# Moving one feed-forward layer of a four-chunk transformer and state-space kernel from beside an attention stage to the kernel's tail

## The chip, the core and the metric

The kernel runs on one core of a Trainium2 chip. The core has five engines, each with its own instruction queue that is worked off in order: TensorE (PE, matmuls; PEld is its loading of weights), VectorE (DVE), ScalarE (ACT), GpSimd (POOL) and SyncE (SP, which issues most of the DMAs here). Data for the engines is in SBUF, and matmul results land in the eight banks of PSUM. The metric is the device time of one execution, in microseconds; lower is better.

## The reference

The input x is float32 of shape (2, 1024, 256): two sequences of 1024 tokens with 256 features. Four layers follow one another, each with a residual:

```python
x = x + attention(layernorm(x))        # 16 heads of 128, causal mask and a linear position bias
x = x + ternary_ffn(layernorm(x))      # silu(gate) * up, 1024 wide, weights at three levels, RMS norm
x = x + mamba(layernorm(x))            # state space: 512 channels, 16 states, recurrence over the tokens
x = x + kept_two_ffn(layernorm(x))     # silu(gate) * up, 1024 wide; of each 4 values the 2 largest stay
```

In the last layer the choice is made by the absolute values of four neighbouring features:

```python
h = silu(x @ w_gate) * (x @ w_up)
h_sparse = sparsify_2to4(h)            # keeps the two of each four with the largest |h|
out = h_sparse @ w_down
```

The recurrence of the third layer is `h = dA * h + dbu`, `y = sum over the states of h * c`, token by token; attention is causal. So the first half of a sequence doesn't depend on the second half, in any layer.

## The kernel before

The tokens are cut into four chunks of 512 (`CH`: two sequences, two halves each; `U` = 512). The residual of a chunk stays in SBUF as `x[k]`. Everything is written in plain Python loops, so the program is one long list of instructions. A scheduler fixes each engine's order before the run: the order in the source is its priority, and it may pull ready work of a later place ahead. It also adds the waits, and hands out buffers: a tile with the tag of an earlier one takes its buffer when the last reader is done.

**Stages.** `attention()` is a generator that yields after each block of 128 queries of a head, 64 times a chunk (16 heads, 4 blocks). `rest(k)` is a second generator with the other three layers of chunk k: `ternary_ffn`, `state_space`, `kept_two_ffn`. The main part at the end of the function interleaves the two: stage 0 is the attention of the first chunk, beside the quantization of weights; in stage k (1 to 3) the attention of chunk k (counted from 0) runs beside `rest(k - 1)`. After stage 3 the attention's pools are closed (`actx.close()`), and `rest(3)` runs alone: the tail.

**Pace.** Each `yield` of `rest` names a cost in planned units. `REST` is their sum, 296.4: 227.6 for the ternary layer and the state space, and 68.8 for the last layer. After block i of 64, `rest` is advanced until it has spent REST * (i + 1) / 64.

**The layer that is moved, `kept_two_ffn` (L671).** It loads three weights of 1 MB each on SP (L679, L681, L683), normalizes and transposes `x[k]` (`layernorm_T`, tile `xT_g`), then for each of 8 pieces calls `glu`: four matmuls for the gate and four for the up half as the profile counts them (L398, tiles `g_g` and `u_g`), a silu on ACT (L403, `sg_g`), and a product on DVE (L404, into `gh`). For every second piece ACT takes absolute values (L700, `ab`). DVE compares these (six comparisons, L706, `cm`), applies four rules (L718, L719, L720: `wins`, `gh`), and the output matmuls (L727, `go`) are added to the residual on DVE (L732, `o`) and stored. All its tiles lie in pools on the right side of SBUF; its PSUM banks come from `ps_r`.

**PSUM.** Two banks with tag s (`ps_s`, attention's scores, and the decay factors of the last chunk's scan), three with tag mm (`ps_mm` and `ps_z`, attention), one y, two r (`ps_r`, shared by all layers of `rest`).

**The state space's scan loop (from L569).** 4 channel groups times 16 states give 64 products. For each one `spread` loads two broadcast rows into `bcs` (512 KB, L576, on SP), `factors` makes the decay `da` on ACT (L593) and the drive `db` (L596: on POOL; in the last chunk two of three on DVE), `scan` runs the recurrence on DVE (L603, `hs`), `weigh` multiplies by the second row on POOL (L614, `hc`), and `total` adds the result into the bank `y` by four PE transposes (L583). `gate` closes a group of 16; at the end `mo` (L663) projects back. `tail_end` is true for the last chunk alone; it selects deeper buffers (`bcs` 8 rather than 5).

Of the kernel before, what the change touches and what calls it, by code (L numbers as in the profile page):

```python
# [9 lines left out]
F32 = mybir.dt.float32  # L10
# [7 lines left out]
P = 128  # L18
B, S, D = 2, 1024, 256
H, DH = 16, 128  # L20
# [5 lines left out]
NFC = FF // P  # L26
GRP = 64
DI, DN, DR, DC = 512, 16, 128, 4
NDC = DI // P
NX = DR + 2 * DN  # L30
U = 512
UT = U // P
# [10 lines left out]
def kernel(  # L43
# [28 lines left out]
    def bank(tag, bufs):  # L72
        return lambda name, dt=F32: ps.tile([P, 512], dt, tag=tag, name=name, bufs=bufs)


    ps_s, ps_mm, ps_z = bank("s", 2), bank("mm", 3), bank("mm", 3)
    ps_y, ps_r = bank("y", 1), bank("r", 2)


    CH = [(b, u) for b in range(B) for u in range(NU)]  # L80
# [18 lines left out]
    def layernorm_T(k, key, put, bank):  # L99

        mv = ln.tile([P, UT, 2], F32, tag="mv", name=f"mv_{key}")
        for i in range(UT):
            st = ln.tile([P, 6], F32, tag="st", name=f"st_{key}_{i}", bufs=3)
            nc.vector.bn_stats(st, x[k][:, i, :])
            nc.vector.bn_aggr(mv[:, i, :], st)
        rstd = ln.tile([P, UT], F32, tag="rstd", name=f"rstd_{key}")
        nc.scalar.activation(rstd, mv[:, :, 1], AF.Sqrt, bias=ln_eps)
        nc.vector.reciprocal(rstd, rstd)
        for i in range(0, UT, 2):
            tp = bank(f"lnp_{key}_{i}").rearrange("p (c t) -> p c t", c=KC)  # L110
            for j in range(2):
                xn = ln.tile([P, D], F32, tag="xn", name=f"xn_{key}_{i}_{j}", bufs=2)
                nc.vector.tensor_scalar(
                    xn, x[k][:, i + j, :], mv[:, i + j, 0:1], rstd[:, i + j : i + j + 1],
                    ALU.subtract, ALU.mult,
                )
                for c in range(KC):
                    nc.tensor.transpose(
                        tp[:, c, j * P : (j + 1) * P], xn[:, c * P : (c + 1) * P], ident
                    )  # L120
            put(slice(i * P, (i + 2) * P), tp)

    def plain(pool, key):
        xT = pool.tile([P, KC, U], F32, tag="xT", name=f"xT_{key}")
        return xT, lambda t, p: nc.any.tensor_copy(xT[:, :, t], p)
# [72 lines left out]
    for h in range(H):  # L198
# [18 lines left out]
        fill=-MASKED, base=0, pattern=[[-1, P]], channel_multiplier=1,  # L217
# [171 lines left out]
    nc.scalar.activation(a_neg, cols_sb[:, :, DC : DC + DN], AF.Exp)  # L389
    nc.vector.tensor_scalar(a_neg, a_neg, -1.0, None, ALU.mult)  # L390

    def glu(pool, key, xTs, g_of, u_of, ic, h):

        g_ps, u_ps = ps_r(f"g_{key}_{ic}"), ps_r(f"u_{key}_{ic}")
        for p, w_of in ((g_ps, g_of), (u_ps, u_of)):
            for c in range(KC):
                for i, xT in enumerate(xTs):
                    nc.tensor.matmul(  # L398
                        p, lhsT=w_of(c, ic), rhs=xT[:, c, :],
                        start=(c == 0 and i == 0), stop=(c == KC - 1 and i == len(xTs) - 1),  # L400
                    )
        sg = pool.tile([P, U], F32, tag="sg", name=f"sg_{key}_{ic}", bufs=2)
        nc.scalar.activation(sg, g_ps, AF.Silu)  # L403
        nc.vector.tensor_tensor(h, sg, u_ps, ALU.mult)  # L404
# [63 lines left out]
    def state_space(k):  # L468
        b, u = CH[k]
        first, last, tail_end = u == 0, u == NU - 1, k == len(CH) - 1  # L470
        ps_da = ps_s if tail_end else ps_r
        with ExitStack() as mctx:
            mc = mctx.enter_context(tc.tile_pool(name="mc", bufs=1, side="right"))
            m2 = mctx.enter_context(tc.tile_pool(name="m2", bufs=2, side="right"))
# [15 lines left out]
            xT, put = plain(mc, f"m{k}")  # L490
# [79 lines left out]
            live, parts, yTs = {}, {0: steps(0)}, {}  # L570
            yield 3

            def spread(i):
                c, n = prods[i]
                live[i] = m2.tile([P, 2, U], F32, tag="bcs", name=f"bcs_{k}_{c}_{n}", bufs=8 if tail_end else 5)
                nc.sync.dma_start(  # L576
                    out=live[i], in_=bcd[:, n, :].unsqueeze(0).to_broadcast([P, 2, U])
                )
# [62 lines left out]
            for i in range(AHEAD):  # L641
                spread(i)
# [17 lines left out]
            for t in range(UT):  # L660
                op = ps_r(f"mo_{k}_{t}")
# [6 lines left out]
                nc.vector.tensor_tensor(xt, xt, op[:, :D], ALU.add)  # L668
                yield 2

    def kept_two_ffn(k):  # L671

        b, u = CH[k]
        W = 2 * U
        with ExitStack() as gctx:
            gc = gctx.enter_context(tc.tile_pool(name="gc", bufs=1, side="right"))
            g2 = gctx.enter_context(tc.tile_pool(name="g2", bufs=2, side="right"))
            wg_sb = gc.tile([P, KC, FF], F32, name=f"wg_sb_{k}")
            nc.sync.dma_start(out=wg_sb, in_=wg.rearrange("(c p) m -> p c m", p=P))  # L679
            wu_sb = gc.tile([P, KC, FF], F32, name=f"wu_sb_{k}")  # L680
            nc.sync.dma_start(out=wu_sb, in_=wu.rearrange("(c p) m -> p c m", p=P))  # L681
            wd_sb = gc.tile([P, NFC, D], F32, name=f"wd_sb_{k}")
            nc.sync.dma_start(out=wd_sb, in_=wd.rearrange("(c p) m -> p c m", p=P))  # L683
            out_dst = out[b, u * U : (u + 1) * U, :].rearrange("(t p) d -> p t d", p=P)
            xT, put = plain(gc, f"g{k}")
            layernorm_T(k, f"g{k}", put, ps_r)
            yield 3
            hT = gc.tile([P, NFC, U], F32, name=f"gh_{k}")
            ab = gc.tile([P, 4, W], F32, name=f"ab_{k}")

            h4 = hT.rearrange("p (j a) t -> p j (a t)", j=4)
            for ic in range(NFC):
                glu(
                    g2, f"g{k}", [xT],
                    lambda c, ic: wg_sb[:, c, ic * P : (ic + 1) * P],
                    lambda c, ic: wu_sb[:, c, ic * P : (ic + 1) * P],
                    ic, hT[:, ic, :],
                )
                if ic % 2:
                    nc.scalar.activation(ab[:, ic // 2, :], h4[:, ic // 2, :], AF.Abs)  # L700
                yield 4

            cm = gc.tile([P, 6, W], BF16, name=f"cm_{k}")
            pairs = [(0, 1), (0, 2), (0, 3), (1, 2), (1, 3), (2, 3)]
            for n, (i, j) in enumerate(pairs):
                nc.vector.tensor_tensor(cm[:, n, :], ab[:, i, :], ab[:, j, :], ALU.is_ge)  # L706
                yield 1.3
            beats = lambda i, j: cm[:, pairs.index((i, j)), :]

            rules = (  # L710
                (beats(0, 1), beats(0, 2), ALU.add, beats(0, 3), ALU.add, ALU.is_ge, 2.0),
                (beats(1, 2), beats(0, 1), ALU.subtract, beats(1, 3), ALU.add, ALU.is_ge, 1.0),
                (beats(2, 3), beats(0, 2), ALU.subtract, beats(1, 2), ALU.subtract, ALU.is_ge, 0.0),
                (beats(0, 3), beats(1, 3), ALU.add, beats(2, 3), ALU.add, ALU.is_le, 1.0),
            )
            for j, (a, c, op_a, d, op_b, cmp, least) in enumerate(rules):
                wins = g2.tile([P, W], BF16, tag="wins", name=f"wins_{k}_{j}")
                nc.vector.tensor_tensor(wins, a, c, op_a)  # L718
                nc.vector.tensor_tensor(wins, wins, d, op_b)  # L719
                nc.vector.scalar_tensor_tensor(  # L720
                    h4[:, j, :], wins, least, h4[:, j, :], op0=cmp, op1=ALU.mult
                )
                yield 2.5
            for t in range(UT):
                op = ps_r(f"go_{k}_{t}")
                for ic in range(NFC):
                    nc.tensor.matmul(  # L727
                        op[:, :D], lhsT=hT[:, ic, t * P : (t + 1) * P], rhs=wd_sb[:, ic, :],
                        start=(ic == 0), stop=(ic == NFC - 1),
                    )  # L730
                o = g2.tile([P, D], F32, tag="o", name=f"o_{k}_{t}", bufs=2)
                nc.vector.tensor_tensor(o, x[k][:, t, :], op[:, :D], ALU.add)  # L732
                nc.sync.dma_start(out=out_dst[:, t, :], in_=o)
                yield 4

    def rest(k):
        yield from ternary_ffn(k)
        yield from state_space(k)
        yield from kept_two_ffn(k)

    REST = 3 + 3 * NFC + 2 * UT + 3 + 4 * NDC + 4 + 3 * NDC + 2.2 * (DN * NDC + 4) + 2 * UT
    REST += 3 + 4 * NFC + 1.3 * 6 + 2.5 * 4 + 4 * UT


    heads = attention()
# [8 lines left out]
            pass  # L754
    for k in range(1, len(CH)):
        r, done = rest(k - 1), 0.0
        for i in range(H * UT):
            next(heads)
            while done < REST * (i + 1) / (H * UT):
                done += next(r, REST)  # L760
        for _ in r:
            pass
    next(heads, None)
    actx.close()
    for _ in rest(len(CH) - 1):
        pass


# [58 lines left out]
```

## Time and profile before

| | us |
|---|---|
| runs of the kernel | 2053.31 median, 2048.87 to 2059.54 |
| the profiled execution, its own time | 2053.75 |
| its span, first to last instruction | 2052.0 |

| engine | busy us | share of the span |
|---|---|---|
| PE | 1758.8 | 86% |
| PEld | 1140.1 | 56% |
| DVE | 1267.5 | 62% |
| ACT | 1039.6 | 51% |
| POOL | 840.3 | 41% |

| stage | attention's exponentials (L334), start of the first to end of the last |
|---|---|
| 0: attention of the first chunk | 20.0 to 239.7 |
| 1 | 253.4 to 780.8 |
| 2 | 792.4 to 1207.3 |
| 3 | 1216.5 to 1731.1 |
| tail: `rest` of the fourth chunk | until 2052.0 |

A row of the timeline reads: start, length, engine, line, operation, output tile, inputs, shapes, count; in square brackets the idle time before it and what ended it. Rows with a count are merged, and their length is the time they cover. In a row of the stretches, busy times follow the order PE, PEld, DVE, ACT, POOL, with the count of instructions; then the granted PE clock as a share of full speed, the DMA engines' busy share, and GB/s. A row of a tile's instructions has the shortest, median and longest duration in ns, and the first and last start. A row of the waits names who waited for whom, for how many us in total, how often, and how long at most. A float32 matmul appears as two records. Stages 1 and 3 hold the second half of a sequence, where a block attends to 5 to 8 blocks of keys; in stages 0 and 2 it is 1 to 4.

### The profile page before, as it was taken

How to read it: one execution, taken by the hardware profiler on the slowest of the kernel's cores; microseconds unless marked ns; L12 is line 12 of the kernel's file. 1: busy time of each engine (PE TensorE's matmuls, PEld its weight loads, DVE VectorE, ACT ScalarE, POOL GpSimd, SP SyncE). 2: the span in 40 equal slices, each digit the busy share in tenths (PEclk: the TensorE clock that was granted, in tenths of full speed). 3: DMA queues.
4: the chain of work that ended last, by engine and by line, in shares of the span. 5: the costliest groups of instructions: out<-in, count | busy, mean ns of one | idle time of the engine just before them, and what ended most of it. 6: DMA issues, size and time to landing. Idle time of an engine off the chain costs nothing. (4 is left out here: it accounts for less than half of the span.)

```text
span 2052.0 us, 22995 instructions
## 1 busy us (share of the span) xinstructions
PE 1758.8 (86%) x7472; PEld 1140.1 (56%) x7472; DVE 1267.5 (62%) x2293; ACT 1039.6 (51%) x1787; POOL 840.3 (41%) x798
## 2 busy tenths in 40 slices
PE   6899999788899999968778999979888999845557
PEld 3566665455556567645556577555555656523334
DVE  6865556566765465657665565566766465367844
ACT  3344475555655546655555547545655463454421
POOL 4510030667762001268773003266776000358740
PEclk9899999899999999988999999999999999865569
DMA  6333433556664113267775142346565211257740
GB/s 194 107 103 106 139 111 96 168 175 169 170 174 139 42 57 118 87 181 193 213 197 171 48 152 76 104 154 184 178 169 159 100 35 32 87 186 215 197 121 11
DMA packets 183400, 272.69 MB, mean 133 GB/s; under 512 B 13152, under 2 KB 87904, under 8 KB 182256
## 3 DMA queue, kind: packets, MB, share of 16 engines
q1 hardware_dynamic: 182128, 258.63, 42.8%
q0 software_dynamic: 1152, 12.58, 1.7%
q8 instruction: 60, 0.98, 0.2%
q14 instruction: 60, 0.49, 0.1%
HBM read 248.82 MB, written 22.35 MB: 132 GB/s over the span
## 5 line engine op out<-in xcount | busy, mean ns | idle before, releaser
L614 POOL TENSOR_TENSOR hc<-hs,bcs 128x512 f32<-128x512 f32 x256 | 346.0, 1359 | 99.9 <-PE y L583 66.6
L321 PE MATMUL s<-kT,qT 128*128 128x512 f32 (+3 forms) x768 | 319.2, 523 | 18.6 <-DVE ss L325 18.6
L596 POOL TENSOR_TENSOR db<-du,bcs 128x512 f32<-128x512 f32 x216 | 284.7, 1323 | 92.4 <-DVE hs L603 40.1
L593 ACT ACTIVATE da<-dl,a_neg 128x512 f32<-128x512 f32 x256 | 175.5, 689 | 257.2 <-DVE hs L603 255.8
L583 PE MATMUL y<-ident,hc 128*128 128x128 f32 x1024 | 188.8, 325 | 129.1 <-POOL hc L614 128.6
L334 ACT ACTIVATE ss<-ss,nm 128x128 f32<-128x128 f32 (+7 forms) x256 | 198.2, 774 | 175.9 <-DVE nm L330 173.9
L263 PE MATMUL z<-pT,v 128*128 128x512 f32 (+3 forms) x768 | 267.2, 496 | 7.1 <-ACT pT L255 6.0
L325 DVE SCALAR_TENSOR_TENSOR ss<-s,lower 128x512 f32<-128x512 f32 (+3 forms) x384 | 203.8, 547 | 107.6 <-PE s L321 104.5
L583 PEld LDWEIGHTS y<-ident,hc 128*128 128x128 f32 x1024 | 141.4, 167 | 167.6 <-POOL hc L614 164.1
L263 PEld LDWEIGHTS z<-pT,v 128*128 128x128 f32 x768 | 146.2, 194 | 147.9 <-issue 102.2
L414 POOL DMA_DIRECT2D guT<-guT_d x4 | 2.5, 628 | 551.5 <-DVE o L732 404.9
L330 DVE CUSTOM_DVE_ANT_0 ss<-ss,alibi 128x128 f32<-128x128 f32 (+7 forms) x256 | 223.6, 880 | 2.9
L252 PE MATMUL pt<-ident,ss 128*128 128x128 f32 x1152 | 186.2, 289 | 44.0 <-DVE x L283 19.7
L255 ACT COPY pT<-pt 128x512 f32<-128x512 f32 (+3 forms) x300 | 133.9, 467 | 173.3 <-PE pt L252 171.5
L603 DVE TENSOR_TENSOR_SCAN hs<-da,db 128x512 f32<-128x512 f32 x128 | 155.6, 1218 | 99.0 <-POOL db L596 80.0
L603 DVE TENSOR_TENSOR_SCAN hs<-da,carry,db 128x512 f32<-128x512 f32 x128 | 162.2, 1277 | 79.0 <-POOL db L596 60.1
L252 PEld LDWEIGHTS pt<-ident,ss 128*128 128x128 f32 x1152 | 146.5, 149 | 101.4 <-ACT pT L255 29.0
L321 PEld LDWEIGHTS s<-kT,qT 128*128 128x128 f32 x768 | 138.3, 206 | 92.8 <-issue 54.4
L301 PEld LDWEIGHTS pv<-wv,xT_a 128*128 128x128 f32 x1024 | 129.1, 198 | 45.4 <-issue 23.2
L283 DVE SCALAR_TENSOR_TENSOR x<-o,rr,x 128x256 f32<-128x256 f32 x256 | 109.4, 475 | 69.8 <-PE o L277 69.7
L301 PE MATMUL pv<-wv,xT_a 128*128 128x128 f32 x1024 | 131.6, 283 | 12.7 <-ACT zs L268 9.5
L277 PE MATMUL o<-wo,zs 128*128 128x256 f32 x512 | 125.4, 383 | 11.5 <-ACT kT L297 9.1
(190 smaller groups left out, 2624.6 us busy)
## 6 DMA issues: line engine op xcount, KB each, us to landing
bcs<-bcd SPq DMA_DIRECT2D x256, 512.0 KB, 5.5
alibi<-alibi_d SPq DMA_DIRECT2D x32, 512.0 KB, 5.9
wq<-in_wqT_dram SPq DMA_DIRECT2D x64, 128.0 KB, 2.5
wk<-in_wkT_dram SPq DMA_DIRECT2D x64, 128.0 KB, 2.4
wv<-in_wvT_dram SPq DMA_DIRECT2D x64, 128.0 KB, 2.4
wo<-in_woT_dram SPq DMA_DIRECT2D x64, 128.0 KB, 2.1
alibi<-alibi_d SPq DMA_DIRECT2D x32, 256.0 KB, 3.4
kd<-kT SPq DMA_DIRECT2D x32, 256.0 KB, 2.4
```

Of the source, the lines that this page charges most:

```text
L252: nc.tensor.transpose(tp[:, i, :], s[:, (kb0 + i) * P : (kb0 + i + 1) * P], ident)
L263: nc.tensor.matmul(zp[:, q0:], lhsT=st["v_all"][:, kb, :], rhs=st["pts"][kb // 4][:, kb % 4, q0:], start=(kb == 0), stop=(kb == last),)
L301: nc.tensor.matmul(vp[:, t, :], lhsT=xT[:, c, t * P : (t + 1) * P], rhs=st["v"][:, c, :], start=(c == 0), stop=(c == KC - 1),)
L321: nc.tensor.matmul(sp[:, :n], lhsT=st["qT"][:, j * P : (j + 1) * P], rhs=st["kT"][:, k0 : k0 + n], start=True, stop=True,)
L325: nc.vector.scalar_tensor_tensor(s[:, k0 : k0 + n], sp[:, :n], CLIP, lower[:, S - W + k0 : S - W + k0 + n], op0=ALU.min, op1=ALU.max,)
L330: nc.vector.tensor_tensor_reduce(out=s[:, :W], in0=s[:, :W], in1=st["alibi"][:, :W], scale=1.0, scalar=3.0e38, op0=ALU.add, op1=ALU.min, a ...
L334: nc.scalar.activation(s[:, :W], s[:, :W], AF.Exp, bias=nm, scale=-1.0, accum_out=st["rs"][:, j : j + 1])
L583: nc.tensor.matmul(yTs[c][:, t * P : (t + 1) * P], lhsT=h[:, t * P : (t + 1) * P], rhs=ident, is_transpose=True, start=start and t == 0, s ...
L593: nc.scalar.activation(da, dl, AF.Exp, scale=a_neg[:, c, n : n + 1])
L596: mul.tensor_tensor(db, du, live[i][:, 0, :], ALU.mult)
L603: nc.vector.tensor_tensor_scan(out=hs, data0=da, data1=db, initial=0.0 if first else carry[:, n, c : c + 1], op0=ALU.mult, op1=ALU.add,)
L614: nc.gpsimd.tensor_tensor(hc, hs, bcs[:, 1, :], ALU.mult)
```

## The change

The last layer of the third chunk, `kept_two_ffn(2)`, leaves stage 3 and runs in the tail, interleaved with `rest(3)`. `END` is 3, the last chunk's index.

- `rest(k)` leaves the last layer out for k = 2. Stage 3 is paced by 227.6 units instead of 296.4; stages 1 and 2 by the same 296.4 as before.
- After the attention's pools are closed, `fill` is the moved layer. Its pools are on the left side of SBUF, in the space of the attention, and its banks are `ps_mm`. After each step of `rest(3)` it is advanced until it has spent LAST / (0.8 * MAMBA) of the units spent there, so that it should be through when `rest(3)` has spent 182 of its 227.6 units before the last layer.
- `bcs` has 6 buffers instead of 8 in the last chunk.

`glu` and `kept_two_ffn` get arguments for the bank and the side; for the other chunks they stay as they were.

```diff
-    def glu(pool, key, xTs, g_of, u_of, ic, h):
-        g_ps, u_ps = ps_r(f"g_{key}_{ic}"), ps_r(f"u_{key}_{ic}")
+    def glu(pool, key, xTs, g_of, u_of, ic, h, bank=ps_r):
+        g_ps, u_ps = bank(f"g_{key}_{ic}"), bank(f"u_{key}_{ic}")
...
-                live[i] = m2.tile([P, 2, U], F32, tag="bcs", name=f"bcs_{k}_{c}_{n}", bufs=8 if tail_end else 5)
+                live[i] = m2.tile([P, 2, U], F32, tag="bcs", name=f"bcs_{k}_{c}_{n}", bufs=6 if tail_end else 5)
...
-    def kept_two_ffn(k):
+    def kept_two_ffn(k, side="right", bank=ps_r):
...
-            gc = gctx.enter_context(tc.tile_pool(name="gc", bufs=1, side="right"))
-            g2 = gctx.enter_context(tc.tile_pool(name="g2", bufs=2, side="right"))
+            gc = gctx.enter_context(tc.tile_pool(name="gc", bufs=1, side=side))
+            g2 = gctx.enter_context(tc.tile_pool(name="g2", bufs=2, side=side))
...
-            layernorm_T(k, f"g{k}", put, ps_r)
+            layernorm_T(k, f"g{k}", put, bank)
...
-                    ic, hT[:, ic, :],
+                    ic, hT[:, ic, :], bank,
...
-                op = ps_r(f"go_{k}_{t}")
+                op = bank(f"go_{k}_{t}")
...
+    END = len(CH) - 1
     def rest(k):
         yield from ternary_ffn(k)
         yield from state_space(k)
-        yield from kept_two_ffn(k)
-    REST = 3 + 3 * NFC + 2 * UT + 3 + 4 * NDC + 4 + 3 * NDC + 2.2 * (DN * NDC + 4) + 2 * UT
-    REST += 3 + 4 * NFC + 1.3 * 6 + 2.5 * 4 + 4 * UT
+        if k != END - 1:
+            yield from kept_two_ffn(k)
+    MAMBA = 3 + 3 * NFC + 2 * UT + 3 + 4 * NDC + 4 + 3 * NDC + 2.2 * (DN * NDC + 4) + 2 * UT
+    LAST = 3 + 4 * NFC + 1.3 * 6 + 2.5 * 4 + 4 * UT
...
     for k in range(1, len(CH)):
         r, done = rest(k - 1), 0.0
+        cost = MAMBA if k == END else MAMBA + LAST
         for i in range(H * UT):
             next(heads)
-            while done < REST * (i + 1) / (H * UT):
-                done += next(r, REST)
+            while done < cost * (i + 1) / (H * UT):
+                done += next(r, cost)
         for _ in r:
             pass
     next(heads, None)
     actx.close()
-    for _ in rest(len(CH) - 1):
-        pass
+    fill, done = kept_two_ffn(END - 1, "left", ps_mm), 0.0
+    used = 0.0
+    for n in rest(END):
+        done += n
+        while used < done * LAST / (MAMBA * 0.8):
+            used += next(fill, LAST)
```

## The prediction

> **What bounds the kernel now.** I read the page's slices first, to find the stages, then the table of busy time by stretch, cut at the points where the timeline changes from one stage to the next. From the slices (each 51.3 us):
>
> ```profile
> PE   6899999788899999968778999979888999845557
> ...
> PEclk9899999899999999988999999999999999865569
> ```
>
> PE is near 9 tenths except in the last six slices. There PE falls to 5 and its clock to 5 or 6 tenths. The stretches (us; then busy us of PE, PEld, DVE, ACT, POOL, the clock, the DMA share, GB/s):
>
> ```profile
> 1216.00:1326.00 110.00, 108.14 (x458) 68.73 (x457) 65.65 (x139) 78.47 (x119) 24.87 (x26) 0.98 0.34 110
> 1326.00:1584.00 258.00, 218.46 (x986) 142.98 (x985) 177.07 (x257) 140.07 (x238) 184.78 (x195) 0.95 0.57 169
> 1584.00:1742.00 158.00, 157.09 (x632) 98.68 (x630) 83.88 (x165) 74.91 (x116) 4.46 (x5) 1.00 0.16 52
> 1742.00:1781.00 39.00, 29.95 (x144) 22.48 (x144) 14.10 (x37) 17.50 (x30) 18.84 (x16) 0.91 0.19 75
> 1781.00:1816.00 35.00, 24.28 (x52) 8.73 (x52) 15.44 (x29) 15.72 (x21) 2.32 (x5) 0.88 0.35 121
> 1816.00:1982.00 166.00, 82.43 (x302) 53.21 (x302) 126.14 (x120) 69.68 (x95) 132.63 (x95) 0.56 0.69 191
> ```
>
> Rows 1 to 3 are stage 3 (attention of chunk 4, with the layers of chunk 3 beside it): up to its first scan, its scans, and the rest, nearly all of it the feed-forward layer that moves. Rows 4 to 6 are the tail: ternary layer (T), input projections (I), scans (M); the last feed-forward layer follows, 70 us. So the layer leaves a stage where PE is the bound and enters one where PE is half idle.
>
> Busy PE is not full PE, so I price matmuls by start to start in the timeline:
>
> ```profile
> 2000.58 1.88 PE L398 MATMUL g_g<-xT_g,wg_sb 128*128 128x512 f32 x4
> 2002.29 1.88 PE L398 MATMUL u_g<-xT_g,wu_sb 128*128 128x512 f32 x4
> ...
> 1703.74 3.62 PE L727 MATMUL go<-wd_sb,gh 128*128 128x256 f32 x16
> 1707.20 1.45 PE L321 MATMUL s<-kT,qT 128*128 128x512 f32 x4
> ```
>
> Four of 512 columns take 1.71 us, 0.429 each; sixteen of 256 take 3.46, 0.216 each; a 128-column one measured likewise 0.109. With these I summed every matmul of a stretch: 197 us of PE work in the 258 of the scans (61 lost), 104 of 110 before them, and some 155 of 158 after them. T has 24 of 39, I 18 of 35, M 38 of 166.
>
> **What stage 3 loses.** The layer's PE work: 64 x 0.429 + 64 x 0.216 + 8 x 0.109 = 42.2 us, in a stretch with no slack, so all of it goes. The second part is the 61 us lost beside the scans. Why are they lost? In stage 2, the same 64 scans ran beside attention that is half as wide:
>
> ```profile
> L603 DVE TENSOR_TENSOR_SCAN hs<-da,carry,db x64: 1253/1282/1285, 888.8 to 1098.5; 128x512 f32<-128x512 f32 x64
> ...
> L603 DVE TENSOR_TENSOR_SCAN hs<-da,db x64: 1184/1223/1225, 1326.2 to 1582.8; 128x512 f32<-128x512 f32 x64
> ```
>
> 211 us there, so the scan chain by itself needs at most 3.3 us a product; in stage 3 it takes 4.03, with only 197 / 64 = 3.1 of PE work. Neither fills the time: each waits for the other. After the change the scans' planned 150 units are spread over 150 / 227.6 x 64 = 42 attention blocks and not 150 / 296.4 x 64 = 32. Ten more blocks of 5.2 us (20.9 us of matmuls a head, four blocks) put PE work at 3.9 to 4.0 a product, above the chain: PE becomes the clear bound and some waits vanish. The PE waits in that stretch were y for hc 12.8 us, s for ss 6.9, pt for pT 5.0 and smaller ones. I take the 12.8 as gone, and half of the 13 us that the clock (0.95) costs; with about 1 us more from the other stretches that is 20. **Stage 3: -42 - 20 = -62 us.** Ends: -45 (the loss stays) and -74 (it halves). Next late there is PE itself.
>
> A rule gives less: the Trainium skill ("Trainium Kernel Development and Optimization", Performance Expectations) says matmul busy time misleads and weight-load busy time is the measure. By it the scans run at 143 / 258 = 0.55 against 98.7 / 158 = 0.62 where PE is full: 29 us lost, of which half would give -57. I keep the pitch sum, since the scans' many 128-column transposes load weights for 0.167 us each against 0.109 of pitch.
>
> **What the tail pays.** The fill is paced by planned units: LN and about three of the eight gate/up pairs in T, three in I, the comparisons, rules and output in M, ending at 0.8 of its units. The scheduler also pulls ready work forward (the first gate's "in" matmuls ran at 1807.8, ahead of the first scan at 1819.6).
>
> T: three pairs are 3 x 8 x 0.429 = 10.3 us of PE, plus LN 0.9. T has 15 us of PE gaps, 6 of them before the ternary weights land and the rest as gaps of 0.8 between its own pairs; two separate banks let the fill use these. I take +5 (0 to 11). Loads: wg, wu, wd are 3 MB more beside guT and prT. If they queue ahead, at the 400 GB/s or so that these loads reached, guT is 7 us late; if they land while the last head still finishes, 0. I take +2. On SP they wait for the attention's last readers (done by 1742); behind them stand the projection weights, due at 1780, so that wait is covered by 38 us. POOL's queue gets nothing new.
>
> I: three pairs, 10.3 us in 16.5 us of gaps, 5 of which are the wait for in_sb: +4 (0 to 10). The silu table is the one already loaded.
>
> M: PE has 128 us free, so 13.8 us of output matmuls (twice that at this clock) cost nothing. ACT has 96 us free; a silu among the exponentials costs two table loads of 1.28 us, with about 2 us of lead: nothing I count. DVE is the question:
>
> ```profile
> DVE hs L603 <- POOL db L596: 27.4, 13, 2.8
> ```
>
> DVE waits for POOL's db, and POOL's hc in turn for DVE's scans (20.3 us). The layer's DVE work here is 18 operations with two SBUF inputs:
>
> ```profile
> L706 DVE TENSOR_TENSOR cm<-ab x6: 1218/1222/1226, 2013.0 to 2029.0; 128x1024 bf16<-128x1024 f32 x6
> L718 DVE TENSOR_TENSOR wins<-cm x4: 682/684/685, 2022.7 to 2034.2; 128x1024 bf16<-128x1024 bf16 x4
> L719 DVE TENSOR_TENSOR wins<-wins,cm x4: 682/684/685, 2030.2 to 2035.4; 128x1024 bf16<-128x1024 bf16 x4
> L720 DVE SCALAR_TENSOR_TENSOR gh<-wins,gh x4: 1216/1216/1217, 2031.4 to 2037.2; 128x1024 f32<-128x1024 bf16 x4
> ```
>
> 6 x 1.22 + 8 x 0.684 + 4 x 1.216 = 17.7 us, timed while POOL was idle. By the busy row DVE has 40 us free in M, so this would be hidden: +0. The rule that speaks against it is in "SBUF — State Buffer", Who interferes with whom: a DVE instruction with two SBUF inputs and a GpSimd instruction reading SBUF exclude each other, the later one blocking fully. The trace agrees:
>
> ```profile
> L596 DVE TENSOR_TENSOR db<-du,bcs x40: 658/666/1762, 1817.7 to 1971.5; 128x512 f32<-128x512 f32 x40
> ...
> 1942.95 1.26 POOL L596 TENSOR_TENSOR db<-du,bcs 128x512 f32<-128x512 f32 x1
> ...
> 1943.15 1.61 DVE L596 TENSOR_TENSOR db<-du,bcs 128x512 f32<-128x512 f32 x1
> ```
>
> The DVE product, 0.67 alone, began just after a POOL product and took 1.61; scans stay at 1.28 beside anything. So count what needs the pair in M: POOL (64 + 24 + 8) x 1.255 = 120.5, DVE 40 x 0.666 + 4 = 31: 151 of 166 us, 91% taken. Adding 17.7 gives 169: at least +3, and +19 at the same fill. If each of the 18 also waits a whole POOL operation on the chain: 17.7 + 18 x 1.26 = 40. I take +16, nearer the fill, since a few comparisons may be pulled ahead of M.
>
> bcs buffers 8 to 6: a load starts when the weighing that frees its buffer ends. From that end to the db six products later the timeline shows 7.4 to 13.5 us once the start-up is over; a load lands in 5.3 us (median, M). Cost 0, 2 us a product if the cover went.
>
> **Tail: 5 + 2 + 4 + 16 = +27.** The profiled execution took 2053.75 us (span 2052.0), 0.4 above the median of the runs: 2053.75 - 62 + 27 = **2019 us**. Its own range is 2005 to 2034.
>
> **Rivals.** (a) More gain: the loss beside the scans halves (-74) and the fill sits in gaps (+10): 1990. For it: the stretch after the scans lost almost nothing; against: the shared pair. (b) The gain is eaten: the two chains keep waiting for each other (-45), the tail takes 11 in T and 25 in the rest (+36): 2045. For it: 4.03 us a product though neither side was full; against: PE's work now exceeds the chain. (c) Slower: the shared pair in M. Every fill operation blocks a POOL product and waits for one (+40), with 16 in T and I, against -45: 2065. It decides as soon as the tail grows by more than stage 3 gives. For it: 91% taken; against: 13 waits for db, up to 2.8 us long, into which an operation can fall.
>
> **Chances.** Forecast 0.62, (a) 0.16, (b) 0.13, (c) 0.09. About 0.5% (10 us) is what can be told from no change. Faster takes the first two and a third of (b): 0.81; same 0.09; slower 0.10. The range 1994 to 2048 leaves out half of (a), most of (c).
>
> **What would show it.** In the new profile: the last exponential of attention near 1670 rather than 1731; 64 stage-3 scans over some 290 to 305 us with PE losing about 45 in them; guT's first matmul about 8 us after the attention ends; M near 182 us, with cm, wins and gh longer than 1.22, 0.68 and 1.22 there; the last 70 us unchanged. I am wrong if stage 3 shrinks by less than 45, if M grows by more than 30, or if db comes to wait for bcs loads.

## The result, and the profile after

The changed kernel took 2033.82 us (median, 2029.05 to 2041.34) beside 2053.22 for the kernel before, a ratio of 0.9905 with a 95% interval of 0.9881 to 0.9929. That is 19.4 us less. The forecast had been 34.75 less, 2019 us; the median lies at the upper edge of the forecast's own range, 2005 to 2034.

The profiled execution of the changed kernel took 2041.34 us, the longest of its runs, and its sum is made against its own time. Here are the slices of its page, the lines that answer to those of before:

```profile
PE   6799999788889999977778999989989998945557
...
PEclk9799999898999999998889999999999999957869
```

The last six slices of PE read almost as before (945557, where it was 845557), but the clock granted in them does not: 957869, where it was 865569. The same busy share at a higher clock is more work done: by pitches, M now holds about 52 us of PE work, where it was 38. The moved matmuls did go into the idle PE of the tail. Now the stretches, with the same columns as before:

```profile
1221.00:1352.00 131.00, 128.13 (x546) 81.55 (x545) 78.65 (x165) 91.20 (x139) 26.88 (x27) 0.99 0.32 101
1352.00:1651.00 299.00, 261.91 (x1166) 167.25 (x1165) 199.44 (x302) 161.42 (x279) 187.94 (x194) 0.95 0.54 155
1651.00:1702.00 51.00, 49.85 (x225) 33.78 (x223) 20.95 (x44) 20.11 (x34) 5.86 (x5) 1.00 0.17 62
1702.00:1744.00 42.00, 35.88 (x143) 25.39 (x142) 16.87 (x44) 21.66 (x38) 18.88 (x15) 0.88 0.22 82
1744.00:1787.00 43.00, 42.30 (x127) 19.64 (x127) 24.95 (x46) 19.63 (x27) 4.71 (x6) 0.96 0.38 117
1787.00:1969.00 182.00, 94.81 (x371) 61.94 (x370) 148.98 (x140) 78.55 (x103) 137.24 (x95) 0.67 0.60 173
1969.00:2040.00 71.00, 55.80 (x169) 33.91 (x168) 30.02 (x48) 11.87 (x17) 0.00 (x0) 0.90 0.15 52
```

The first three rows are stage 3: before the scans, beside them, after them. The next three are T, I and M, and the last is the chunk's own last layer. The tail's 64 scans, whose first start and last end are taken as M below, before and after:

```profile
L603 DVE TENSOR_TENSOR_SCAN hs<-da,carry,db x64: 1248/1282/1284, 1819.6 to 1976.3; 128x512 f32<-128x512 f32 x64
...
L603 DVE TENSOR_TENSOR_SCAN hs<-da,carry,db x64: 1250/1272/1284, 1790.7 to 1963.5; 128x512 f32<-128x512 f32 x64
```

Cut at the instructions themselves (first exponential, first and last scan, the attention's last matmul), the two profiles compare so:

| part | before, us | after, us | difference | forecast |
|---|---|---|---|---|
| start of stage 3 | 1216.5 | 1221.5 | +5.0 | 0 |
| stage 3 | 524.6 | 481.3 | -43.3 | -62 |
| T and I | 78.5 | 87.9 | +9.4 | +11 |
| M | 158.0 | 174.0 | +16.0 | +16 |
| last layer and end | 74.4 | 74.8 | +0.4 | 0 |

These add to -12.5 by the rounded rows; the two executions differ by 12.4. The 5.0 us ahead of stage 3 are not put down to the change: every engine has the same instructions in the same order up to there in both kernels. Without them the change is worth -43.3 + 25.8 = -17.5 us in the profiles, close to the 19.4 of the medians. So the tail cost what was forecast, and stage 3 gave about 19 us less than forecast.

**Where the gain in stage 3 went.** By start-to-start pitches, PE's work in stage 3 fell from 456.5 to 413.7 us (such sums are good to about 1 us). That is the layer's own 42.8, and the stage became just that much shorter. So the time PE loses stayed nearly as it was: beside the scans it was 61.1 us and is now 57.9 (299 less 241 of work). Of this PE stood idle for 39.5 us before and 37.1 after (258 less 218.46 busy, 299 less 261.91). Who is PE waiting for there? First the waits of PE beside the scans, before (1326 to 1584 us):

```profile
PE y L583 <- POOL hc L614: 12.8, 8, 2.4
PE s L321 <- DVE ss L325: 6.9, 6, 2.3
```

and after (1352 to 1651 us):

```profile
PE s L321 <- DVE ss L325: 20.1, 15, 3.8
```

The wait of `y` for `hc` is gone from the list, as forecast. In its place the scores `s` wait for DVE to empty a score bank (`ss`), and for 13 us more than before. DVE works its queue in order, so a late scan can hold up the `ss` behind it; the runs below show how much of this wait that explains. What makes a scan late? The waits of POOL in the same stretches, first before:

```profile
POOL hc L614 <- PE y L583: 22.1, 12, 7.3
...
POOL db L596 <- DMA bcs<-bcd: 7.1, 6, 3.1
```

and after:

```profile
POOL hc L614 <- PE y L583: 53.7, 13, 8.6
POOL db L596 <- DMA bcs<-bcd: 30.8, 21, 3.5
```

Two things are to be seen. POOL waits 53.7 us for PE to take its products, so PE did become the side that is waited for more. But the drive `db` now waits 30.8 us for the broadcast rows, in 21 places rather than 6. The loads come from SP, which waits in order for buffers. Its own waits after, beside the scans:

```profile
SPq L576 <- POOL hc L614: 101.3, 40, 6.4
SPq L576 <- POOL carry L616: 51.4, 19, 5.3
SPq L242 <- PE z L263: 35.7, 9, 9.8
SPq L230 <- PE o L277: 26.0, 10, 7.4
```

L576 is the load of `bcs`; it waits for one of five buffers, whose last reader is the weighing `hc` (or the `carry` behind it). L242 and L230 are loads of the attention's weights. They wait up to 9.8 us at the head of the same queue, with the next `bcs` load behind them. With more attention blocks beside the scans there are more of these (9 and 10 waits, 61.7 us, where before it was 5 and 8, 41.3 us, the longest 13.3). That they are what makes the `bcs` loads late is a reading of the queue; no run separates it from buffers that come free later.

### The profile page after: what moved, and what is told of

Its sections match the earlier page's. It is cut to its first block, busy times and chain, and to the rows that moved or that the text cites. A ratio compares the mean times of both kernels' runs of the same rounds, so it can differ in the third digit from the quotient of the medians.

```text
span 2039.6 us, 22970 instructions
## 1 busy us (share of the span) xinstructions
PE 1756.2 (86%) x7472; PEld 1138.6 (56%) x7472; DVE 1277.2 (63%) x2291; ACT 1036.0 (51%) x1787; POOL 854.8 (42%) x798
## 3 DMA queue, kind: packets, MB, share of 16 engines
q1 hardware_dynamic: 182128, 258.63, 42.8%
## 5 line engine op out<-in xcount | busy, mean ns | idle before, releaser
L263 PE MATMUL z<-pT,v 128*128 128x512 f32 (+3 forms) x768 | 275.7, 509 | 11.8 <-ACT pT L255 8.0
L583 PE MATMUL y<-ident,hc 128*128 128x128 f32 x1024 | 181.7, 315 | 119.6 <-POOL hc L614 118.8
L330 DVE CUSTOM_DVE_ANT_0 ss<-ss,alibi 128x128 f32<-128x128 f32 (+7 forms) x256 | 229.3, 902 | 2.7
L583 PEld LDWEIGHTS y<-ident,hc 128*128 128x128 f32 x1024 | 136.4, 161 | 158.7 <-POOL hc L614 153.1
L301 PEld LDWEIGHTS pv<-wv,xT_a 128*128 128x128 f32 x1024 | 126.2, 195 | 41.3 <-issue 23.4
```

The source lines that it names most:

```text
L263: nc.tensor.matmul(zp[:, q0:], lhsT=st["v_all"][:, kb, :], rhs=st["pts"][kb // 4][:, kb % 4, q0:], start=(kb == 0), stop=(kb == last),)
L301: nc.tensor.matmul(vp[:, t, :], lhsT=xT[:, c, t * P : (t + 1) * P], rhs=st["v"][:, c, :], start=(c == 0), stop=(c == KC - 1),)
L330: nc.vector.tensor_tensor_reduce(out=s[:, :W], in0=s[:, :W], in1=st["alibi"][:, :W], scale=1.0, scalar=3.0e38, op0=ALU.add, op1=ALU.min, a ...
L583: nc.tensor.matmul(yTs[c][:, t * P : (t + 1) * P], lhsT=h[:, t * P : (t + 1) * P], rhs=ident, is_transpose=True, start=start and t == 0, s ...
```

## The experiments

Each ratio below is against runs of the kernel before that were timed beside that kernel, so two changed kernels are compared by their ratios. In the five kernels below whose stage 3 is that of the changed kernel, the exponentials there take 468.1 to 471.3 us, and in the changed kernel 471.3: differences of about 3 us say nothing in stage 3.

Theories for stage 3: **(S1)** late `bcs` loads keep the forecast 20 us from appearing; **(S2)** two chains in order on shared engines lose about 60 us beside the scans whatever the loads do. For the tail: **(P1)** the +16 of M is that DVE operations with two SBUF inputs and POOL's products shut each other out, by the SBUF port that they share; **(P2)** it is DVE's own time, in a chain that DVE and POOL alternate in; **(B)** part of it is the two buffers less.

**Buffers alone.** The kernel before with one line changed:

```diff
-    live[i] = m2.tile(..., name=f"bcs_{k}_{c}_{n}", bufs=8 if tail_end else 5)
+    live[i] = m2.tile(..., name=f"bcs_{k}_{c}_{n}", bufs=6 if tail_end else 5)
```

> The kernel before with 6 bcs buffers in the last chunk and nothing else of the change. If the buffers cost nothing (theory): 2053 us within 4, and the tail's 64 scans take 158 us from the first to the end of the last, as before. If the buffers are what lengthened the tail's scans (rival): those scans take 168 us or more and the time is 2063 or more.

Measured: 2057.99 us beside 2055.53, ratio 1.0011 [1.0003, 1.0020]; M is 161.1 us where it was 158.0. So the buffers cost 2 to 3 us (0.6 to 4 by the interval), where the prediction had nothing. How is not shown: no operation waits for a `bcs` load in this M either, and DVE's and POOL's queues came out in another order.

**No loads in stage 3.** In the third chunk the first five `bcs` tiles are read again in turn, so 59 loads are left out:

```diff
+                if k == 2 and i >= 5:
+                    live[i] = ring[i % 5]
+                    return
                 live[i] = m2.tile([P, 2, U], F32, tag="bcs", ...)
+                ring.append(live[i])
```

> The change, with the bcs tiles of the third chunk loaded five times only and then used again for the other 59 products (so the third chunk's state space gets wrong rows; no load is waited for after the fifth). Theory: the db products that wait for bcs loads (30.8 us beside the stage-3 scans, 7.1 before the change) hold the scans, the ss operations behind them on DVE, and PE's scores: stage 3, from the first exponential to the end of the last, falls from 471 us to about 451, the time to about 2014. Rival, the loads are off the path and the loss beside the scans is one of order and banks: stage 3 stays within 6 us of 471 and the time at 2030 to 2038.

Measured: 2026.79 us, 0.9858 [0.9844, 0.9872]. The attention's exponentials in stage 3 take 459.8 us rather than 471.3, where the theory had 451. PE's largest wait beside the scans is now

```profile
PE s L321 <- DVE ss L325: 14.9, 14, 2.2
```

and 46.5 us are lost there. So S1 is right for about 11 us, and S2's 60 is less than 50 without the loads. The other 9 of the 20 don't come back even where no load exists, and `s` still waits 8 us more for `ss` than before the change: late loads explain 5 us of the 13 that this wait grew by.

**A sixth buffer.** It has to be paid for: the fourth chunk's residual takes the space of the first chunk's, which is long stored, and is loaded when stage 3 begins.

```diff
-        x.append(const.tile([P, UT, D], F32, name=f"x{k}"))
+        x.append(const.tile([P, UT, D], F32, tag="x", name=f"x{k}", bufs=len(CH) - 1))
...
-    live[i] = m2.tile(..., name=f"bcs_{k}_{c}_{n}", bufs=6 if tail_end else 5)
+    live[i] = m2.tile(..., name=f"bcs_{k}_{c}_{n}", bufs=6 if k >= 2 else 5)
```

> The change, with the fourth chunk's residual in the buffer of the first chunk's (loaded when the fourth chunk's attention begins), and the 4 KB so freed used for a sixth bcs buffer in stage 3. If late bcs loads are what stage 3 loses by (theory): about half of the 20 us comes back, stage 3 about 461 us, the time about 2024; the waits of db for bcs beside the stage-3 scans fall from 30.8 to below 15. Rival: no change against the changed kernel's 2034, within 4.

Measured: 2029.15 us, 0.9869 [0.9853, 0.9885], and the exponentials of stage 3 take 461.6 us. POOL's waits for the loads beside the scans (the lines of this file are shifted by seven):

```profile
POOL db L603 <- DMA bcs<-bcd: 8.5, 6, 1.8
```

One buffer brings nearly all that leaving the loads out brings. As a control, the shared residual with five buffers as in the changed kernel:

> The change with the fourth chunk's residual in the first chunk's buffer and no other edit, as a control for the sixth bcs buffer. If the gain of x3_bcs6 came from the buffer (theory): stage 3 near 470 us and the time 2030 to 2037, as the changed kernel. If it came from the shared residual or a different order (rival): stage 3 near 462, the time near 2028.

Measured: 2042.86 us, 0.9930 [0.9903, 0.9956]; stage 3's exponentials take 471.0 us and `db` waits 35.1 us for the loads. So the gain of the kernel above is the buffer's. (With it POOL's `hc` and `db` also came in another order, DVE's queue in the same; what that order alone is worth was not tried.)

**Deeper products.** If POOL's 53.7 us behind `y` are what makes the scans late, more `hc` buffers should let POOL run ahead. First with five `bcs` buffers, then with six (in the second, the attention's `xT` is down to one buffer to make the room):

```diff
-    hc = m2.tile(..., name=f"hc_{k}_{c}_{n}", bufs=5 if tail_end else 3)
+    hc = m2.tile(..., name=f"hc_{k}_{c}_{n}", bufs=5 if k >= 2 else 3)
```

> The change, with the fourth chunk's residual in the first chunk's buffer, and the 4 KB used for five hc buffers instead of three in stage 3 (bcs stays at 5 there). Beside the stage-3 scans POOL's hc waited 54 us for PE's y in the changed kernel, up to 9 us at a time. If this wait passes on through POOL and DVE to PE's scores (theory): stage 3 falls from about 469 us to 462 or less, the time to about 2027. Rival: PE sets the pace and hc merely waits for its turn; stage 3 within 3 us of 469, the time 2030 to 2037.

> The change with six bcs and five hc buffers in stage 3; the space comes from the shared residual buffer and from a single buffer for the attention's transposed input. If loads and hc are two separate waits (theory): stage 3 at about 453 us, the time about 2021. If only the loads count (rival): as with six bcs buffers alone, stage 3 about 461 us, the time about 2029.

Measured: 2041.52 us, 0.9944 [0.9928, 0.9960], and 2037.38, 0.9920 [0.9902, 0.9939]. Stage 3's exponentials take 477.3 and 468.1 us, beside 471.0 and 461.6 with three buffers. Neither is faster for it, and with six `bcs` buffers the kernel is slower. The waits of the first one show what happens (POOL, 1352 to 1652 us, lines shifted by seven):

```profile
POOL db L603 <- DVE hs L610: 48.6, 9, 18.5
POOL hc L621 <- PE y L590: 39.0, 12, 8.6
```

POOL no longer waits so long for PE, but it now waits 48.6 us for scans (4.2 in the changed kernel), once for 18.5 us. The scheduler had put a different order into the queues, so these two kernels are more than the one edit. They say that these deeper queues didn't bring the missing 9 us, and not where these are. What speaks against the theory without them is POOL's wait for `y` in the faster kernels: 73.0 us with a sixth `bcs` buffer and 77.6 without loads, longer than the 53.7.

**No rules in the moved layer.** The comparisons, the `wins` and their products into `gh` are left out of the fill, 18 DVE operations of 17.7 us; its pace stays.

> The change, with the comparisons and rules of the moved layer left out (18 DVE operations with two SBUF inputs, 17.7 us alone; the third chunk keeps all values instead of two of four). If these lengthen the tail's scans (theory, the shared port and DVE's time): the scans fall from 174 us to about 158 and the time to about 2018. If something else of the fill does (its output matmuls, its silus, the six buffers): they stay above 168 and the time above 2028.

Measured: 2020.95 us, 0.9829 [0.9812, 0.9846]; M takes 160.3 us. So 13.7 of M's 16.0 are these operations, and the 2.3 that are left are about what the buffers cost. Its scans:

```profile
L603 DVE TENSOR_TENSOR_SCAN hs<-da,carry,db x64: 1249/1282/1284, 1783.0 to 1942.1; 128x512 f32<-128x512 f32 x64
```

In the changed kernel the rows of these tiles in the tail were (ns, shortest, median, longest):

```profile
L706 DVE TENSOR_TENSOR cm<-ab x6: 1195/1224/2282, 1757.5 to 1828.7; 128x1024 bf16<-128x1024 f32 x6
...
L719 DVE TENSOR_TENSOR wins<-wins,cm x4: 661/1098/1758, 1835.3 to 1878.3; 128x1024 bf16<-128x1024 bf16 x4
L720 DVE SCALAR_TENSOR_TENSOR gh<-wins,gh x4: 1195/1746/2287, 1843.4 to 1880.1; 128x1024 f32<-128x1024 bf16 x4
```

Three of the six comparisons ran ahead of the scans, at 1.2 us. The longest of each kind is about 1.1 us above its time alone, a little less than one POOL operation of 1.26. Of the 16 operations that ran inside M six were stretched, by 5.4 us together. In the timeline of DVE:

```profile
1843.36 2.29 DVE L720 SCALAR_TENSOR_TENSOR gh<-wins,gh 128x1024 f32<-128x1024 bf16 x1
1845.57 1.75 DVE L596 TENSOR_TENSOR db<-du,bcs 128x512 f32<-128x512 f32 x1
```

and of POOL in the same microseconds:

```profile
1843.00 1.56 POOL L614 TENSOR_TENSOR hc<-hs,bcs 128x512 f32<-128x512 f32 x1 [0.24 <-DVE hs L603]
1844.52 2.25 POOL L596 TENSOR_TENSOR db<-du,bcs 128x512 f32<-128x512 f32 x1
```

`gh` began while `hc` ran and came out 1.07 us longer than its 1.22; then POOL's `db` began while `gh` ran and took 2.25 rather than 1.26; then DVE's own `db` took 1.75 rather than 0.67. Each waits for the one that began first. But longer operations alone don't separate P1 from P2, since these operations cost DVE their own time too. The next two kernels are to separate them.

**The port alone.** Both put the same ten DVE operations (six comparisons, four products with `h4`; the `wins` are left out, and the values compared are others) in the place of the rules. In the first both inputs lie in SBUF; in the second one input is a PSUM bank that ACT has filled:

```diff
-    nc.vector.tensor_tensor(cm[:, n, :], ab[:, n % 3, :], ab[:, 3, :], ALU.is_ge)
...
+    nc.scalar.copy(pb, ab[:, 3, :U])
+    over = pb.unsqueeze(1).to_broadcast([P, 2, U])
...
+    nc.vector.tensor_tensor(two(cm[:, n, :]), two(ab[:, n % 3, :]), over, ALU.is_ge)
```

(`two` cuts a row of 1024 into two of 512; the products take `over` in the same way.)

> The change with the moved layer's rules cut down to six comparisons and four products on DVE (12.2 us alone), all with two SBUF inputs; the eight wins operations are left out, so the third chunk's choice is wrong. The tail's scans took 160 us without any such operation and 174 with all 18. Both theories of the tail expect some 168 to 171 us here and a time near 2028.

> As lock_sbuf, ten operations of the same shapes, but one input of each lies in PSUM, so that each reads SBUF once (the comparisons are against values that have no meaning). If what they cost is the shared SBUF port with POOL (theory): the tail's scans take 160 to 164 us and the time is near 2021. If it is DVE's own time in its queue (rival): 167 us or more, within 2 of lock_sbuf.

Measured: 2020.34 us, 0.9845 [0.9815, 0.9875], and 2016.05, 0.9820 [0.9803, 0.9837]; M takes 164.1 and 155.4 us, both less than the theories had (168 to 171, and 160 to 164). The rows with both inputs in SBUF:

```profile
L728 DVE TENSOR_TENSOR cm<-ab x6: 1194/2150/2311, 1798.7 to 1829.1; 128x1024 bf16<-128x1024 f32 x6
...
L614 POOL TENSOR_TENSOR hc<-hs,bcs x64: 1252/1393/2347, 1779.6 to 1942.5; 128x512 f32<-128x512 f32 x64
```

and with one in PSUM:

```profile
L732 DVE TENSOR_TENSOR cm<-ab,pb x6: 1191/1200/1209, 1805.7 to 1827.2; 128x1024 bf16<-128x1024 f32 x6
...
L614 POOL TENSOR_TENSOR hc<-hs,bcs x64: 1253/1268/1716, 1783.5 to 1937.6; 128x512 f32<-128x512 f32 x64
```

The same comparison, beside the same POOL work, has a median of 2.15 us with two SBUF inputs and 1.20 with one of them in PSUM; POOL's median product goes from 1.39 to 1.27. That shows P1's mechanism: the two shut each other out when both of DVE's inputs lie in SBUF. Nothing of P2 is seen for these ten: 12 us of DVE work with a PSUM input leave M no longer than none at all (155.4 beside 160.3). The size is less sure. That an M with ten operations more is 5 us shorter means that M moves by about so much with the order of its queues, and the timed intervals of the two kernels overlap. With two SBUF inputs the ten cost 3.8 us over none and 8.7 over the PSUM kernel; neither is a measured price of the port, and how the 13.7 of all 18 divide between P1 and P2 stays open.

**An earlier fill.** The pace's 0.8 is made 0.4, so the rules run before the scans begin:

```diff
-        while used < done * LAST / (MAMBA * 0.8):
+        while used < done * LAST / (MAMBA * 0.4):
```

> The change with the fill due at 0.4 instead of 0.8 of the fourth chunk's units, so that its rules stand ahead of most of the scans, where POOL has little to do. If the rules cost only what POOL and DVE lock each other out of (theory): the tail's scans fall from 174 to about 162 us and what comes ahead of them in the tail grows by less than that (88 to some 95): about 2030. If the stretch ahead of the scans has no room on PE and DVE (rival): it grows by 12 us or more and the time is 2034 or above.

Measured: 2035.66 us, 0.9899 [0.9876, 0.9923]. The comparisons are not stretched:

```profile
L706 DVE TENSOR_TENSOR cm<-ab x7: 1215/1219/1226, 1738.6 to 1999.6; 128x1024 bf16<-128x1024 f32 x7
```

(the seventh is the fourth chunk's own). All 18 rules of the fill now stand ahead of the scans, and M falls from 174.0 to 161.8, as long as with six buffers and no fill (161.1). But T and I rise from 87.9 to 100.3, which is the rival: 12.2 us are saved and 12.4 are paid, so nothing is gained. With the rules, 9 us of output matmuls moved ahead of the scans too; which of them fill T and I was not tried.

**Together.** The sixth buffer in stage 3, seven in the last chunk, and the fill's comparisons in halves with one input in PSUM, where ACT writes the absolute value instead of leaving it in SBUF:

```diff
-    live[i] = m2.tile(..., name=f"bcs_{k}_{c}_{n}", bufs=6 if tail_end else 5)
+    live[i] = m2.tile(..., name=f"bcs_{k}_{c}_{n}", bufs=(5, 5, 6, 7)[k])
...
+    nc.scalar.activation(pb, h4[:, base, a : a + U], AF.Abs)
+    nc.vector.tensor_tensor(cm[:, n, a : a + U], of(i), of(j), ALU.is_ge)
```

(`of` gives the bank `pb` for the value that ACT put there and the SBUF tile for the other.)

> A version meant to beat both: the change with six bcs buffers in stage 3 and seven in the tail (residual buffer shared, as in x3_bcs6), and with the moved layer's comparisons reading one of their two inputs from PSUM, where ACT writes those absolute values; twelve operations of 512 instead of six of 1024, 8 us alone. By the shared-port theory the tail's scans fall from 174 us to about 168 and the time to about 2023; by the rival (no room on DVE or ACT for more operations) the scans stay at 172 or more and the time at 2028 or more.

Measured: 2019.77 us, 0.9820 [0.9799, 0.9841], faster than the kernel before, the changed one (0.9905 [0.9881, 0.9929]) and the sixth buffer alone (0.9869 [0.9853, 0.9885]). Stage 3's exponentials take 461.3 us and M 164.7. The comparisons in the tail:

```profile
L724 DVE TENSOR_TENSOR cm<-ab,ab x12: 654/658/678, 1801.3 to 1826.2; 128x512 bf16<-128x512 f32 x12
```

Twelve halves, none of them longer than 0.68 us in the middle of the scans. M's 9 us less than the sixth buffer alone (173.6) come with two edits at once, the seventh buffer and the PSUM input, and aren't divided between them. A last kernel adds a seventh buffer in stage 3 too, with one `xT` buffer in the attention:

> bcs6_cm_psum with a seventh bcs buffer in stage 3, for which the attention's transposed input has a single buffer. db still waited 8.5 us for loads with six. If loads are the wait (theory): stage 3 falls by 2 to 4 us more, the time to 2015 to 2019. If the single buffer of the transposed input or another order costs more than that (rival): 2021 or above.

Measured: 2017.47 us, 0.9820 [0.9789, 0.9851], the same as with six within the intervals; stage 3's exponentials take 460.0 us. Six are enough.

## Why the prediction was right and wrong

**Stage 3's PE work, -42: right.** The pitch sums fell by 42.8 us.

**Stage 3's loss, -20: this step failed.** It read: "I take the 12.8 as gone, and half of the 13 us that the clock (0.95) costs; with about 1 us more from the other stretches that is 20." The 12.8 did go. But the loss did not shrink with it, since another wait took its place: `s` for `ss` rose from 6.9 to 20.1 us. The clock's half, 6.5 us, had no reason beside it, and the clock beside the scans stayed at 0.95 (0.96 without loads). Stage 3 gave 43.3 in all, 0.5 more than the work that left it. That is below the forecast's own end for "the loss stays", -45, which its terms don't give: 42 of work and no loss won back is -42. The reasoning was that PE's work per product (241 / 64 = 3.8 us measured, 3.9 to 4.0 forecast) would stand above the scan chain's 3.3 and PE would become the clear bound. The chain's 3.3 came from stage 2, where half as much attention ran beside it. Spread over 299 us, the chain took 4.67 a product: five `bcs` buffers were no longer enough, at 10 to 11 us, as leaving out the loads and adding a buffer both show. That was named as a sign of being wrong ("if db comes to wait for bcs loads"), and so was a stage 3 that shrinks by less than 45; both came, but the cost of the first was not in the sum. About 9 us of the 20 are missing without any load too, and more `hc` buffers didn't bring them. In size they are little more than the clock's 6.5 and the 1 of the other stretches, but what they are is not shown, nor why `s` still waits 14.9 us for `ss` there.

The prediction's other measure, weight-load time, would have given 15 of loss to win rather than 20. It is nearer by its figure, but what was won is nothing to speak of, so neither measure says what a loss shared by two chains gives back.

**T, I and the loads, +11: right in size (+9.4), not in its parts.** All eight gate/up pairs ran in T and I, not six, and by the rows of the stretches, cut by eye, T grew by 3 and I by 8, where T with the loads was to grow by 7 and I by 4. The first matmul with `guT` came 7.8 us after the attention's end (8 forecast). Most of the pairs fitted into PE's gaps: the eight are 8 x 8 x 0.429 = 27.5 us of PE work.

**M, +16: right in sum, with two small errors against each other.** The operations cost 13.7 and not 16, the buffers 2 to 3 and not 0. That the sum came out at 16.0 is luck, the more so as M moves by some 5 us with the order of its queues. The row of busy times alone (40 us of DVE free) would have put these at nothing; the rule of the Trainium skill ("SBUF — State Buffer", Who interferes with whom), that DVE with two SBUF inputs and a GpSimd instruction reading SBUF exclude each other, is what gave the size. The two kernels with ten operations of equal shapes agree with the rule: 2.15 us against 1.20. They don't show that the size came by it alone. The reading of the wait was only partly right: DVE's waits for `db`, into which operations might fall, shrank from 27.4 to 19.9 us, and POOL's for the scan grew from 20.3 to 37.4. Before, and then after:

```profile
POOL hc L614 <- DVE hs L603: 20.3, 33, 1.7
...
POOL hc L614 <- DVE hs L603: 37.4, 31, 3.6
...
DVE hs L603 <- POOL db L596: 19.9, 9, 3.0
```

**The rivals.** The result is the stage 3 of rival (b), whose loss stays, with the tail of the forecast. Rival (c), every operation of the fill blocking and being blocked for +40, has its mechanism in the rows above and a third of its price. Rival (a) didn't show. So the time came out inside the forecast's range with 20 us of it missing: the work that left stage 3, and the tail's cost, were sized well enough to carry it.

## What to carry to other kernels

A wait that goes from an engine's list frees time only if nothing else is nearly as late: before its length is counted as gain, ask for the next buffer, load and queue on the same chain at the new rate, here five load buffers that held at 31 blocks beside the scans and not at 40. Time that two chains lose to each other need not shrink when one of them becomes the clear bound: here it stayed at about 60 us. When vector work is moved beside busy GpSimd work, count its SBUF inputs as well as its time, and see whether one of them can come from PSUM.

## What the runs showed of the hardware that was not expected

- A DVE operation of 1.2 us with two SBUF inputs took up to 2.3 us beside POOL; the same with one PSUM input stayed within 1.19 to 1.21, and POOL's products beside it were shorter as well. The scan, which has its decay in PSUM, stayed at 1.25 to 1.29 in the tail of every kernel.
- 12 us more of DVE work with a PSUM input made M no longer (155.4 us, beside 160.3 without it).
